# A two-layer graph kernel: final stores in source order, one weight requested by SyncE, and two weights' digit copies stored by SyncE

## The chip, the cores and the metric

The kernel runs on one core of one Trainium2 chip. That core has TensorE (PE) for matmuls, VectorE (DVE) and ScalarE (ACT) for elementwise work, GpSimd (POOL), and SyncE (SP), which in this kernel only asks for transfers. DMAs are asked for by SP, by POOL and, a few times, by ACT. The metric is the device time of one execution in microseconds (us). The kernel before was timed three times: 2391.77, 2391.25 and 2391.67 us, median 2391.67 us.

## The reference

The input x has 64 samples of 256 rows and 512 features, and all samples share one 256 x 256 adjacency matrix of zeros and ones. Layer 0 is masked attention with 8 heads, layer 1 is a product with the adjacency and then with a weight. Each ends in a residual sum and a layer norm:

```python
q, k, v = x @ Wq + bq, x @ Wk + bk, x @ Wv + bv          # 8 heads of 64
scores = q @ k.T / sqrt(64) + (1 - adj) * -1e9
x = layernorm(x + softmax(scores) @ v @ Wo + bo)
x = layernorm(x + (adj @ x) @ weight + bias)
```

## The kernel before, in words

**Tiling.** The samples are worked on in pairs, 32 pairs in all (`NP`); a pair `p` is 512 rows. Every fp32 matrix product with a weight is computed as three products of shortened operands, called digits: `high`, `low` and `diff`. A weight's digits are made once: ACT makes `high` (`split_high`, L118), DVE makes `low` and `diff` (`split_rest`, L123 and L124), and ACT scales `low` at the end (`split_scale`, L127). They are made in a ring of six SBUF tiles called `wr`, of 1 MB each, three for one weight at a time, so two weights can be there at once. From there `keep` (L129) stores each digit tile to a DRAM scratch buffer, and for all later pairs `load_w` (L105) loads them back into the ring, stage after stage. The names of the stages are `qk0`, `qk1`, `v`, `o` and `l`; `o` is the weight Wo (argument `wo`) and `l` is layer 1's weight (argument `w1`).

**Order of the work.** The issue order of PE, DVE, ACT and POOL is the order of the source: they are named in `tc.manual_schedule` (L764). Inside it `start()` handles pair 0, `first(w)` and `second(w)` are the two halves of the loop over pairs, where work on pair `w`, on pair `w - 1` and preparations for pair `w + 1` are mixed, and `ending()` handles the last pair with what remains of the one before. SP is not named there. The planner decides on its order, with its own estimates of when things are ready.

**What SP asks for.** Rows of x for the next pair come in blocks through `load_x` (L75), four DMAs of 64 KB for one block, each made of runs of 128 bytes; DVE transposes each block (`x_t`, L274). The blocks 0 and 1 of pair 1 go to tiles named `x`, the blocks 2 and 3 to tiles named `o`. The residual rows come through `load_r` (L83, 1 MB). The raw weight of layer 1 comes through `load_l` (L214). Finished rows go out at L547 and, for the last pair, at L545.

**What POOL asks for.** All loads and stores of weight digits, four DMAs of 256 KB for the raw Wo (`load_o`, L208, called at L705 in the middle of `start()`), and DMAs that add a bias to the residual rows on the way (L495, in the first and the last pairs). POOL also computes the power of minus one half in the layer norms (L523 and L595).

**Where the moved transfers are used.** Raw Wo is read first by PE at L241 (`bv_wo`, a product of the v bias with Wo), then by ACT at L118 when the digits of `o` are made in `first(1)`. The ring tiles that hold the digits of `o` are written again in `second(1)`, when the digits of `l` are made (L118 under `second(1)`); that can happen only when the stores of the `o` digits have landed. Likewise, the tiles of `l` are loaded again with `qk1` of pair 2 once the stores of `l` have landed.

**The last pair.** Its four row blocks of layer 1 are normalized by `normed` (L530): block 0 and block 2 by ACT, block 1 by DVE, and block 3 half by ACT and half by DVE. Blocks 0 to 2 and the right half of block 3 are stored by SP, the left half of block 3 by ACT. The planner has SP ask for them in the order block 1, block 0, right half of block 3, block 2. After that, all engines read a small count from memory (L782) and branch on it; the branch skips a general fallback version of the kernel. A barrier of all engines (L956) ends the program.

Of the kernel before, what the change touches and what calls it, by code (L numbers as in the profile page):

```python
# [8 lines left out]
F32 = mybir.dt.float32  # L9
# [6 lines left out]
P = 128  # L16
# [19 lines left out]
def fast(tc, x, adj, wq, bq, wk, bk, wv, bv, wo, bo, w1, b1, out):  # L36
# [6 lines left out]
    nc = tc.nc  # L43
    B, N, D = x.shape
    HD = D // H
    DC = D // P
    NC = N // P
    NP = B // 2
    HF = D // 2
# [12 lines left out]
    two = pool("two", 2)  # L62
# [8 lines left out]
    RAW, SCRATCH, W, UNCUT, BEGUN = {}, {}, {}, {}, {}  # L71
# [3 lines left out]
    def load_x(p, i):  # L75

        if p < NP:

            t = XC[p, i] = two.tile([P, D], F32, name="o" if p == 1 and i > 1 else "x")
            for q in range(4):  # L80
                nc.sync.dma_start(t[q * 32:(q + 1) * 32].rearrange("i (m j) -> i m j", j=32), xb[p, i, q])

    def load_r(p):  # L83
        if p < NP:
            t = two.tile([P, 2, NC, D], F32, name="r")
            nc.sync.dma_start(t, xr[p])
            R[p] = [t[:, b] for b in range(2)]
# [41 lines left out]
    def keep(name, i, part):  # L129

        SCRATCH[name, i] = scratch.tile([P, 2, 2, D], F32, name=f"{name}{i}")
        nc.gpsimd.dma_start(SCRATCH[name, i], part.bitcast(F32))

    def in_ring(f, name, p, k):

# [58 lines left out]
    for k in range(DC):  # L194
        RAW["v", k] = four.tile([P, D], F32, name="high")
        nc.sync.dma_start(RAW["v", k], wv[k * P:(k + 1) * P])
    for i in range(4):
        load_x(1, i)
    bo_s, b1_s = on_all(bo, "bo"), on_all(b1, "b1")

    def small_ones():
# [2 lines left out]
        nc.gpsimd.memset(first_of_32, 0.0)  # L204
        for d in range(DC):
            nc.gpsimd.memset(first_of_32[d * 32:d * 32 + 1], 1.0)

    def load_o(k):  # L208
        if k % 2 == 0:
            RAW["o"] = two.tile([P, 2, D], F32, name="hl")  # L210
        RAW["o", k] = RAW["o"][:, k % 2]
        nc.gpsimd.dma_start(RAW["o", k], wo[k // 2 * HF:(k // 2 + 1) * HF].rearrange("(h a i) e -> a h i e", h=4, a=2)[k % 2])

    def load_l():  # L214
        t = two.tile([P, DC, D], F32, name="r")
# [226 lines left out]
    def scores(p, g, between=[]):  # L442
        if not 0 <= p < NP:
            return
        for b in range(2):
            for kc in range(NC):

                sc = [banks.tile([P, 2, N], F32, name="ps") for s in range(2)]
                keys = slice(b * N + kc * P, b * N + (kc + 1) * P)
                for a in range(2):  # L450
                    digits = (1, 0, 2) if (p, g) != (0, 0) else (0,)
                    for i in digits:
                        for s in range(2):
                            r = slice(s * HD, (s + 1) * HD)
                            nc.tensor.matmul(sc[s][:, a, :], K[p, g][r, a, i, keys], Q[p, g][r, a, i, b * N:(b + 1) * N],  # L455
                                             start=i == digits[0], stop=i == digits[-1])
                if (p, g) == (NP - 1, 1):

                    names = (("x", two), ("high", four), ("low", four), ("diff", four))
                    name, pool_of = names[2 * b + kc]  # L460
                    e = [pool_of.tile([P, 2, N], F32, name=name) for _ in range(2)]
                    whole = []
                else:
                    e = one.tile([P, 2, 2, N], F32, name=f"e{2 * b + kc}")
                    whole, e = [e.rearrange("p s a n -> p (s a) n")], [e[:, s] for s in range(2)]
                E[p, g, b, kc] = e, whole
                if (b, kc) == (1, 1):
                    do(*between)
                for s in range(2):
                    nc.scalar.activation(e[s], sc[s], AF.Exp, scale=(RHO if (p, g) != (0, 0) else 1.0) * qscale)  # L470
# [15 lines left out]
    def masks(p, g, b):  # L486
        return [(masked, p, g, b, 0), (masked, p, g, b, 1), *([(summed, p, g, b)] if (p, g) != (NP - 1, 1) else [])]
# [145 lines left out]
    def do(*tasks):  # L633
        for t in tasks:
            for f, *args in (t if isinstance(t, list) else [t]):
                f(*args)
# [31 lines left out]
    def second(w):  # L668
        q, n = w - 1, w + 1
        high, rest, scale = ([(f, "l", 0, k) for k in range(DC if w == 1 else 0)] for f in (ring_high, ring_rest, ring_scale))  # L670
        values(w, 0, ([(squared, q, "o", 2), (hl_low, q, 0, 0), (hl_low, q, 0, 1), *high[:1]], [(squared, q, "o", 3), *high[1:2]]))
        scores(w, 1)
        m = masks(w, 1, 0) + masks(w, 1, 1)
        if w == 1:

            m = [high[2:] + rest[:2], m[:1] + scale[:1] + rest[2:], m[1:2] + scale[1:], m[2:3], m[3:4], m[4:]]
        else:
            m = [m[:3], m[3:4], m[4:5], [], m[5:], []]
        do((inverse, q, "o", 1), (with_b1, q, 0), m[0],
           (block, "q", n, 0), (less, q, "o", 1), (normed, q, "o", 2), (normed, q, "o", 3), m[1],  # L680
           (adj_x, q, 0, 0), (hl_high, q, 1, 0), (hl_low, q, 1, 0), m[2],
           (block, "k", n, 0), (adj_x, q, 0, 1), (hl_high, q, 1, 1), (hl_low, q, 1, 1),
           (qk_high, "q", n, 0), (qk_rest, "q", n, 0), (qk_high, "k", n, 0), (qk_rest, "k", n, 0), m[3],
           (block, "q", n, 1), (adj_x, q, 1, 0), (k_low, n, 0), (qk_high, "q", n, 1), m[4],
           (block, "k", n, 1), (stage_end, n), (adj_x, q, 1, 1), (qk_high, "k", n, 1), (qk_rest, "q", n, 1),
           m[5][:1], (block, "l", q, 0), (qk_rest, "k", n, 1), (k_low, n, 1), m[5][1:], (block, "l", q, 1), (with_b1, q, 1),
           (mean, q, "l", 0), (squared, q, "l", 0), (squared, q, "l", 1), (o_high, w, 0, 0), (o_high, w, 1, 0),
           (inverse, q, "l", 0), (o_rest, w, 0, 0), (block, "l", q, 2), (less, q, "l", 0), (o_rest, w, 1, 0),
           (block, "l", q, 3), (mean, q, "l", 1), (stage_end, q))
# [6 lines left out]
    def start():  # L696
        make_identity(nc, ident)
        do(*((x_first, i) for i in range(4)), (biases,), *((x_high, 0, i) for i in range(4)), (small_ones,))
        qk1, v = (steps_of(*stage) for stage in STAGES[:2])
        high, rest, scale = ([(f, "qk0", 1, k) for k in range(DC)] for f in (ring_high, ring_rest, ring_scale))  # L700
        do((block, "q", 0, 0), (x_rest, 0, 0), (x_rest, 0, 1), qk1[0], (block, "k", 0, 0), (x_rest, 0, 2), (x_rest, 0, 3),
           qk1[1], (block, "q", 0, 1), qk1[2], v[0], (block, "k", 0, 1), v[1][:1], (x_t, 1, 0),
           (adj_t,), qk1[3])
        scores(0, 0)
        do(v[1][1:], (x_t, 1, 1), masks(0, 0, 0), (block, "q", 0, 2), v[2], *((load_o, k) for k in range(DC)), (qk_high, "q", 0, 2), (qk_rest, "q", 0, 2), v[3], (test_adj,),  # L705
           (block, "k", 0, 2), (x_high, 1, 0), (x_high, 1, 1), (qk_high, "k", 0, 2), (qk_rest, "k", 0, 2), masks(0, 0, 1),
           (block, "q", 0, 3), (k_low, 0, 2), (qk_high, "q", 0, 3), (qk_rest, "q", 0, 3), (x_rest, 1, 0), (x_t, 1, 2),
           (block, "k", 0, 3), (stage_end, 0), (qk_high, "k", 0, 3), (qk_rest, "k", 0, 3), (x_rest, 1, 1), (x_t, 1, 3), high[:2],
           (block, "v", 0, 0), (x_high, 1, 2), high[2:], (k_low, 0, 3), (block, "v", 0, 1), (x_rest, 1, 2),
           (block, "v", 0, 2), (x_high, 1, 3), (x_rest, 1, 3), (block, "v", 0, 3), (stage_end, 0), (load_r, 0), (load_l,))  # L710
        values(0, 0)
        scores(0, 1)
        do((bv_wo,), rest[:2], scale[:1], rest[2:3], scale[1:2], rest[3:], scale[2:])
        qk0 = [(f, name, 1, j) for j in range(2) for name in "qk" for f in (qk_high, qk_rest)]
        m = masks(0, 1, 0) + masks(0, 1, 1)
        do((begun, "q", 1, 0), (begun, "k", 1, 0), (block, "q", 1, 0), m[:4], qk0[:2], (block, "k", 1, 0), m[4:5], qk0[2:4], m[5:],
           (block, "q", 1, 1), (k_low, 1, 0), qk0[4:6], (o_high, 0, 0, 0), (o_high, 0, 1, 0), (o_rest, 0, 0, 0),
           (with_bv,), (block, "k", 1, 1), qk0[6:], (stage_end, 0), (k_low, 1, 1), (o_rest, 0, 1, 0))
# [42 lines left out]
           (last_variance,), (root, 1), (less, p, "l", 1, c1), (normed, p, "l", 3, D // 2))  # L761

    PE, DVE, ACT, POOL = mybir.EngineType.PE, mybir.EngineType.DVE, mybir.EngineType.Activation, mybir.EngineType.Pool
    with tc.manual_schedule(engines={PE, DVE, ACT, POOL}):  # L764
        start()
        first(1, steps_of("o", 0))
        second(1)
        load_r(1)
        for w in range(2, NP - 1):
            first(w)  # L770
            second(w)
        ending()

    good = one.tile([P, 2, N // 32], F32, name="z")
# [186 lines left out]
```

## Time and profile before

| what | value |
|---|---|
| median of three timed runs | 2391.67 us |
| the profiled execution's own time | 2391.06 us |
| its span, first to last instruction | 2389.2 us |
| PE busy | 2374.3 us (99%) |
| DVE / ACT / POOL busy | 83% / 63% / 19% of the span |
| granted TensorE clock | 0.999 |
| DMA, mean over the span | 608.70 MB, 255 GB/s |
| DMAs asked for by POOL (q0) / by SP (q1) | 57.5% / 20.4% of 16 engines' span |
| first matmul starts / last matmul ends | 3.77 us / 2379.23 us |

The profile is of one execution, so a sum made from its rows is to be set against that execution's 2391.06 us; 1.86 us of it lie outside the span. Matmuls are pipelined and their ends are modelled, so PE's busy time alone doesn't say that it never waits: gaps between the starts of matmuls, and the waits that the views list, have to be read beside it. In the views of single instructions the columns are start, duration, engine, line, operation and tiles, and, in brackets, how long the engine stood idle and who ended it.

### The profile page before, as it was taken

How to read it: one execution, taken by the hardware profiler on the slowest of the kernel's cores; microseconds unless marked ns; L12 is line 12 of the kernel's file. 1: busy time of each engine (PE TensorE's matmuls, PEld its weight loads, DVE VectorE, ACT ScalarE, POOL GpSimd, SP SyncE). 2: the span in 40 equal slices, each digit the busy share in tenths (PEclk: the TensorE clock that was granted, in tenths of full speed). 3: DMA queues.
4: the chain of work that ended last, by engine and by line, in shares of the span. 5: the costliest groups of instructions: out<-in, count | busy, mean ns of one | idle time of the engine just before them, and what ended most of it. 6: DMA issues, size and time to landing. Idle time of an engine off the chain costs nothing.

```text
span 2389.2 us, 43002 instructions
## 1 busy us (share of the span) xinstructions
PE 2374.3 (99%) x16925; PEld 1907.5 (80%) x16925; DVE 1991.0 (83%) x3311; ACT 1505.4 (63%) x2793; POOL 443.5 (19%) x755
## 2 busy tenths in 40 slices
PE   9999999999999999999999999999999999999998
PEld 6788887888878888878888788887888878888776
DVE  7988888888888888888988888888888888888867
ACT  6666666566565665666656656666566665666655
POOL 1222111111111111121111112111111111121121
PEclk9999999999999999999999999999999999999999
DMA  9897788777888777887777967788778887777782
GB/s 295 274 310 244 265 255 283 259 230 256 260 265 271 241 237 256 264 293 238 236 255 254 310 240 224 265 255 286 258 227 261 261 264 268 238 244 255 256 274 62
DMA packets 373651, 608.70 MB, mean 255 GB/s; under 512 B 272316, under 2 KB 275908, under 8 KB 313156
## 3 DMA queue, kind: packets, MB, share of 16 engines
q0 software_dynamic: 71632, 500.21, 57.5%
q1 hardware_dynamic: 301104, 105.29, 20.4%
q8 instruction: 135, 2.21, 0.4%
q14 instruction: 72, 0.59, 0.1%
q10 hardware_dynamic: 708, 0.40, 0.1%
HBM read 551.29 MB, written 49.28 MB: 251 GB/s over the span
## 4 chain that ended last, share of the span: by engine, by line
PE 96%; DVE 1%; ACT 0%; issue 0%; POOLq 0%; ACTq 0%
PE ps L339 72%; PE ps L421 9%; PE ps L455 8%; PE ps L615 5%; PE ps L411 3%; DVE e L476 0%; DVE wr L124 0%; DVE wr L123 0%; PE ps L565 0%; DVE kT L389 0%; DVE qT L387 0%; DVE qT L385 0%; ACT kT L394 0%; DVE kT L385 0%; ACT waste L517 0%
## 5 line engine op out<-in xcount | busy, mean ns | idle before, releaser
L373 ACT ACTIVATE uncut<-ps,numbers 128x512 f32<-128x512 f32 x252 | 174.0, 690 | 274.0 <-PE ps L339 218.1
L476 DVE TENSOR_TENSOR e<-e,adjT 128x1024 f32<-128x1024 f32 x252 | 299.3, 1219 | 0.2 <-ACT e L470 0.2
L339 PE MATMUL ps<-low,wr 128*128 128x512 f32 x992 | 271.6, 395 | 0.0
L339 PE MATMUL ps<-wr,sl 128*128 128x512 f32 x1008 | 270.6, 390 | 0.1
L339 PE MATMUL ps<-wr,sh 128*128 128x512 f32 x1008 | 269.8, 389 | 0.0
L339 PE MATMUL ps<-wr,sd 128*128 128x512 f32 x1008 | 269.4, 389 | 0.0
L339 PE MATMUL ps<-high,wr 128*128 128x512 f32 x992 | 266.4, 390 | 0.0
L339 PE MATMUL ps<-diff,wr 128*128 128x512 f32 x992 | 265.0, 389 | 0.0
L523 POOL TENSOR_TENSOR ln<-ln,numbers 128x2 f32<-128x2 f32 x127 | 140.4, 1105 | 667.0 <-DVE ln L522 621.3
L470 ACT ACTIVATE e<-ps 128x512 f32<-128x512 f32 x504 | 253.3, 629 | 8.6 <-PE ps L455 8.6
L517 ACT ACTIVATE waste<-r,ln 128x512 bf16<-128x512 f32 x255 | 184.0, 722 | 104.6 <-DVE ln L510 98.9
L421 PE MATMUL ps<-e,v 128*32 128x256 f32 x4032 | 229.1, 379 | 0.0
L538 ACT ACTIVATE r<-r,ln 128x512 f32<-128x512 f32 x254 | 193.7, 811 | 55.1 <-DMA x<-in_x_dram 29.9
L339 PEld LDWEIGHTS ps<-wr,sh 128*128 128x128 f32 x1008 | 189.3, 188 | 39.9
L339 PEld LDWEIGHTS ps<-wr,sd 128*128 128x128 f32 x1008 | 189.2, 188 | 39.5 <-DMA wr<-o 0.2
L339 PEld LDWEIGHTS ps<-high,wr 128*128 128x128 f32 x992 | 186.2, 188 | 41.9 <-ACT e L470 0.8
L339 PEld LDWEIGHTS ps<-diff,wr 128*128 128x128 f32 x992 | 186.2, 188 | 39.1
L339 PEld LDWEIGHTS ps<-wr,sl 128*128 128x128 f32 x1008 | 186.9, 188 | 38.2 <-issue 0.4
L455 PEld LDWEIGHTS ps<-qT,kT 64*128 64x128 f32 x3056 | 187.8, 187 | 27.1 <-PE ps L421 12.4
L385 DVE SCALAR_TENSOR_TENSOR qT<-qT,uncut 128x512 fp32r<-128x512 f32 x126 | 86.8, 689 | 146.9 <-ACT qT L378 146.8
L339 PEld LDWEIGHTS ps<-low,wr 128*128 128x128 f32 x992 | 177.7, 188 | 35.5 <-ACT wr L127 0.6
L455 PE MATMUL ps<-qT,kT 64*128 64x256 f32 x3056 | 201.6, 285 | 0.5 <-ACT kT L394 0.5
(166 smaller groups left out, 4156.1 us busy)
## 6 DMA issues: line engine op xcount, KB each, us to landing
wr<-qk POOLq DMA_DIRECT2D x183, 1024.0 KB, 7.6
wr<-v POOLq DMA_DIRECT2D x93, 1024.0 KB, 6.8
wr<-o POOLq DMA_DIRECT2D x90, 1024.0 KB, 7.8
wr<-l POOLq DMA_DIRECT2D x90, 1024.0 KB, 8.6
r<-in_x_dram SPq DMA_DIRECT2D x32, 1024.0 KB, 12.0
out_dram<-r SPq DMA_DIRECT2D x62, 512.0 KB, 2.9
x<-in_x_dram SPq DMA_DIRECT2D x488, 64.0 KB, 5.4
qk<-wr POOLq DMA_DIRECT2D x6, 1024.0 KB, 8.3
```

The lines of the kernel that those rows point to most:

```text
L339: nc.tensor.matmul(pm, *pairs[k][i], start=i == 0 and k == 0, stop=i == n - 1 and k == DC - 1)
L373: nc.scalar.activation(to, pm, AF.Identity, bias=bias[:, j:j + 1], scale=scale)
L385: nc.vector.scalar_tensor_tensor(low, high.bitcast(F32), -RHO, UNCUT.pop((name, p, j)), op0=OP.mult, op1=OP.add)
L411: nc.tensor.matmul(at[h * 32:(h + 1) * 32, b, :], ones, chunk[h], start=i == 0, stop=i == len(sm) - 1)
L421: nc.tensor.matmul(at[h * 32:(h + 1) * 32, a, :], V[p, b][:, kc, col:col + 32], E[p, g, b, kc][0][h % 2][:, h // 2, :], start=kc == 0, sto ...
L455: nc.tensor.matmul(sc[s][:, a, :], K[p, g][r, a, i, keys], Q[p, g][r, a, i, b * N:(b + 1) * N], start=i == digits[0], stop=i == digits[-1])
L470: nc.scalar.activation(e[s], sc[s], AF.Exp, scale=(RHO if (p, g) != (0, 0) else 1.0) * qscale)
L476: nc.vector.tensor_tensor(e, e, mask[:, kc:kc + 1, :].to_broadcast([P, e.shape[1], N]), op=OP.mult)
L517: nc.scalar.activation(waste, R[p][b][:, c], AF.Square, bias=t[0][:, c:c + 1], accum_out=t[1][:, c:c + 1])
L523: nc.gpsimd.tensor_tensor(t[2], t[1], power[:, cs], op=OP.pow)
L538: nc.scalar.activation(r[:, :cut], r[:, :cut], AF.Identity, scale=scale, bias=bias)
L615: nc.tensor.matmul(pm[:, j, :], t[:, i, mc, j * P:(j + 1) * P], adjT[:, mc, :], start=mc == 0 and i == 0, stop=mc == NC - 1 and i == 1)
```

## The change

It has three parts. `keep` sends the digit stores of the stages `o` and `l` (six DMAs of 1 MB, once each in the program) to SP instead of POOL. The four DMAs of raw Wo are asked for by SP, ahead of all loops, between the blocks 0 and 1 and the blocks 2 and 3 of pair 1's rows, and `load_o` goes. `ending()` stands in a schedule of its own that also names SP, so that SP's order there is the source's too; the planner keeps SP's order everywhere before.

```diff
     def keep(name, i, part):
 
         SCRATCH[name, i] = scratch.tile([P, 2, 2, D], F32, name=f"{name}{i}")
-        nc.gpsimd.dma_start(SCRATCH[name, i], part.bitcast(F32))
+        (nc.sync if name in "ol" else nc.gpsimd).dma_start(SCRATCH[name, i], part.bitcast(F32))
...
-    for i in range(4):
+    for i in range(2):
+        load_x(1, i)
+    for k in range(DC):
+        if k % 2 == 0:
+            RAW["o"] = two.tile([P, 2, D], F32, name="hl")
+        RAW["o", k] = RAW["o"][:, k % 2]
+        nc.sync.dma_start(RAW["o", k], wo[k // 2 * HF:(k // 2 + 1) * HF].rearrange("(h a i) e -> a h i e", h=4, a=2)[k % 2])
+    for i in range(2, 4):
         load_x(1, i)
...
-    def load_o(k):
-        if k % 2 == 0:
-            RAW["o"] = two.tile([P, 2, D], F32, name="hl")
-        RAW["o", k] = RAW["o"][:, k % 2]
-        nc.gpsimd.dma_start(RAW["o", k], wo[k // 2 * HF:(k // 2 + 1) * HF].rearrange("(h a i) e -> a h i e", h=4, a=2)[k % 2])
...
-        do(v[1][1:], (x_t, 1, 1), masks(0, 0, 0), (block, "q", 0, 2), v[2], *((load_o, k) for k in range(DC)), (qk_high, "q", 0, 2), (qk_rest, "q", 0, 2), v[3], (test_adj,),
+        do(v[1][1:], (x_t, 1, 1), masks(0, 0, 0), (block, "q", 0, 2), v[2], (qk_high, "q", 0, 2), (qk_rest, "q", 0, 2), v[3], (test_adj,),
...
+    SP = mybir.EngineType.SP
     with tc.manual_schedule(engines={PE, DVE, ACT, POOL}):
         start()
         first(1, steps_of("o", 0))
...
             first(w)
             second(w)
+    with tc.manual_schedule(engines={PE, DVE, ACT, POOL, SP}):
         ending()
```

In the changed build the issue order of PE and ACT is the same as before. On POOL the ten moved DMAs are gone and the rest stands in the same order. On SP the four Wo DMAs and six digit stores come in, and the last four stores are in the order block 0, block 1, block 2, right half of block 3. On DVE two neighbours change places once, where `ending()` begins: the mean of a block of layer 1 (L510) now comes after a transpose (L428) instead of before it.

## The prediction

> **What bounds the kernel now.** I read the page's header, busy shares and chain first, then the waits by engine, then PE's gaps in stretches, and last the instructions that use what the moved DMAs bring.
>
> ```profile
> span 2389.2 us, 43002 instructions
> ...
> PE 2374.3 (99%) x16925; PEld 1907.5 (80%) x16925; DVE 1991.0 (83%) x3311; ACT 1505.4 (63%) x2793; POOL 443.5 (19%) x755
> ...
> PE 96%; DVE 1%; ACT 0%; issue 0%; POOLq 0%; ACTq 0%
> ```
>
> The chain that ended last is PE's own work for 96% of the span. Matmul starts agree with that: from the first matmul at 3.77 us to the last end at 2379.23 us, PE is without one for only 1.14 us in all. So a change of DMA queues can win at most about 1.1 us inside this stretch, and something at its end (9.97 us from 2379.23 to 2389.2); it can lose whatever it delays beyond its cover. The waits of PE between 4 and 80 us name what is left there:
>
> ```profile
> PE ps L261 <- DMA low<-in_x_dram: 4.1, 2, 3.8
> PE ps L455 <- ACT kT L394: 0.5, 1, 0.5
> ```
>
> The first is the first x rows, which are asked for before anything that moves. The second ends a stretch in which DVE is busy without a pause from 54 to 74 us, working, not waiting for a transfer.
>
> The moved transfers, from the page's list of DMA issues (queue, KB each, median us to landing), with two of SP's for comparison:
>
> ```profile
> r<-in_x_dram SPq DMA_DIRECT2D x32, 1024.0 KB, 12.0
> ...
> o<-wr POOLq DMA_DIRECT2D x3, 1024.0 KB, 5.9
> l<-wr POOLq DMA_DIRECT2D x3, 1024.0 KB, 9.8
> ...
> low<-in_x_dram SPq DMA_DIRECT2D x4, 256.0 KB, 4.2
> ...
> hl<-in_L_gnn_Wo_dram POOLq DMA_DIRECT2D x4, 256.0 KB, 13.0
> ```
>
> And the instructions that first need what they touch, from the timeline: the transpose of pair 1's block 2 (block 3's is at 45.49), PE's first use of Wo, ACT's first write of an `l` digit into the ring, and DVE's sum that needs a bias added by DMA.
>
> ```profile
> 42.24 0.71 DVE L277 STREAM_TRANSPOSE xT<-o 128x512 f32<-128x512 f32 x1
> 55.71 1.06 PE L241 MATMUL ps<-hl,numbers 128*32 128x512 f32 x8
> 113.50 0.62 ACT L118 ACTIVATE wr<-r 128x512 fp32r<-128x512 f32 x1
> 147.03 0.69 DVE L360 SCALAR_TENSOR_TENSOR r<-ps,r 128x512 f32<-128x512 f32 x1
> ```
>
> No bracket stands behind any of them: none waited.
>
> **What the Trainium skill says.** DMA: Bandwidth & Descriptors, section "Issuing engines are not separate DMA queues": DMAs of SP, ACT and POOL run on the same 16 engines, and another issuer saves only the issuing time. So the moves don't add bandwidth. The trace agrees: the DMA share is about 1.0 in every 5 us from 5 to 60 us, whoever asks. Its section "Queues, rings and completion order": each DMA engine goes round robin between the queues, a packet at a time. The trace fits: 8 KB packets of POOL's queue take 310 to 390 ns, 128 B packets of SP's 14 to 20 ns, and SP's 64 KB row pieces land after 10.9 to 16.3 us where POOL's queue is full: 32 packets per engine, each waiting for a large one, is about 11 us. A queue with small packets is thus slow beside POOL's, and that is the risk in moving stores to SP.
>
> **Part 1, Wo by SP.** POOL loses four issues of 0.69 us (32.60 to 35.31), and its store of the last `v` digit, behind them, goes out at about 32.7 instead of 35.28. It landed at 49.59, and the reload of that tile after it (50.10) was followed by PE's use at 77.23: 17 us of cover, so nothing comes of it. On SP the four stand ahead of blocks 2 and 3, bo, b1 and pair 2's blocks 0 and 1. Wo itself landed by 47.05, for a use at 55.71; now asked for at about 18.8, it lands by about 32. What is late next is x: in 2 KB packets of SP's queue (90 to 116 ns) 1 MB is 512 packets, on 16 engines 2.9 to 3.7 us alone; with POOL's packets between, about 9 us. Block 2 landed at 27.27 and moves to 30 to 37, needed at 42.24; block 3 from 32.32 to 35 to 41, needed at 45.49. At least 4.5 us are left. Without that cover each us is DVE's, which has 1.2 + 0.8 us of idle time at 49 to 54, and then PE's. bo (33.13) is needed at 71.8; pair 2's blocks (49.33 and 55.08) at 75.1, and they gain from Wo's leaving POOL's queue in front of them. Sum: 0.
>
> **Part 2, six digit stores by SP.** POOL loses six issues of about 0.55 us; behind them stand reloads that wait for PE to end a stage (97.8 and 130.2), so they go no earlier. SP is idle when the stores become ready: the `o` digits at 91.4, 95.4 and 96.6 (SP's row pieces before are issued by 90.67, the next wait for DVE until 104.73), the `l` digits at 121.6, 123.9 and 126.6. Behind these last stands pair 1's residual load, issued at 122.93 before and at about 127.1 now; it is needed at 164.5, 12 us or even 20 us after issue is early. The price of an 8 KB row on SP's queue isn't in the trace. Lower bound: it is one packet as on POOL's, and the third `o` store lands by about 105. Upper bound: it is cut to 2 KB, 32 packets per engine and store, against the 24 packets per engine of the three reloads from 99.8 us on: 24 rounds of 0.42 us end at about 110, the rest takes 0.7 us, so it lands at about 111.5. ACT needs the tile at 113.50. I take 108. Sum: 0, with 2 us of cover at the worst. For `l`, the reloads of that ring part come at 146.04; the stores land by 142 even if slow. Sum: 0.
>
> **Part 3, the end.** The order of SP's last stores becomes block 0 (ready 2379.71), 1 (2378.96), 2 (2380.97), right half of 3 (2381.72).
>
> ```profile
> 2378.98 3.94 SPq L545 DMA_DIRECT2D out_dram<-r  x4
> ...
> 2381.94 0.38 ACTq L545 DMA_DIRECT2D out_dram<-r  x1
> ```
>
> In this row before, the four issues are at 2378.98, 2379.74, 2381.75 and 2382.12; block 2 is the last, lands at 2385.41, and SP is through with its semaphores at 2386.66. New: 2379.74, 2380.1, 2381.0, 2381.75, and the last is 128 KB, as the one that landed at 2383.75. ACT's half lands at 2384.31 as before. SP would be through about 0.8 to 1.1 us earlier. But the trace also has POOL's DRAIN, from 2381.61 for 6.48 us to 2388.09, and only then the barrier opens. That one covers SP's gain wholly, unless it waits for the last store, which nothing shows. Bounds 0 and -0.9; I take -0.2.
>
> The changed place on DVE is at 2287.17: the mean (0.17) now follows the transpose (0.70), so ACT's square after it goes from 2287.43 to about 2288.0, and ACT's next two evictions move by 0.6 us, the second to an end at 2290.5. PE needs its bank for the fourth pair of score products, at 2288.64 + 3 x 0.77 = 2290.95. 0.4 us of cover. Sum: 0.
>
> Total: -0.2 us on the profiled execution's 2391.06, that is 2390.9; on the median, 0.6 higher, 2391.5. About 0.2% (4.8 us) is what a measurement can tell from no change.
>
> **Rivals.**
> 1. POOL's DRAIN follows the last landing (it ends 2.68 us after it). For: nothing else explains its length; the DRAIN at the start took 0.18. Against: it starts right after POOL's own last semaphore. Then 0.5 to 0.9 us are gained: 2391.0.
> 2. A store lands late and takes the place of what it freed (slower). Place: ACT at 113.50 waits for the third `o` store; behind it stand the evictions at 114.03 and 115.73, and PE's fourth score pair at about 116.9 needs the second (ended 116.32), so it decides from a landing at about 114.0 and then costs 1 us for 1 us. Rows that land late for 42.24 have the same form, from about 44. For: 64 KB pieces on SP took up to 20 us to land at 34 to 54. Against: the DMA engines have the same bytes to move as before and were done with this group at 112.8. If they lose 1 to 3 us: 2392.5 to 2394.5; slower by 0.2% needs a landing at 119.
> 3. The bias DMA before 147.03 landed at 146.93; queued now beside SP's stores and residual load it may land 1 us later, and PE's score pairs reuse that bank at about 148.75, 1.0 us after the sum ends. So up to 0.5 us: 2391.9. That it lands earlier gives nothing.
> 4. The 0.46 us of PE at 74 us, and the rest of the 1.14, go: 2390.6. Against: DVE's work there is the same.
>
> That the change doesn't do what it says is no rival: the issue orders of the two builds differ in just these places.
>
> **How the numbers follow.** Nothing reaches the end: 0.55, own range 2391.1 to 2392.0 (the runs spread over 0.52). Rival 1: 0.18. Rival 2: 0.12, of it 0.03 beyond 4.8 us. Rival 3: 0.08. Rival 4: 0.04. That an unseen effect of the shifted queues in the regular rounds costs more than 4.8 us: 0.02, that it gains as much: 0.01. Range 2390.4 to 2393.0: it leaves out rival 2's upper half and the unseen effects. Faster by over 0.2%: 0.01; within: 0.94; slower: 0.05.
>
> **What would show it.** PE busy 2374 us with gaps of about 1.1 us; no bracket behind the four instructions quoted above; Wo landed before 35 us; the `o` stores landed before 113; SP's four last issues between 2379.7 and 2382.1 with POOL's DRAIN still near 6.5 us. A DRAIN shorter by SP's gain is rival 1. I am wrong if ACT waits at L118 near 113.5, DVE at L277 near 42, or if PE shows gaps that recur in every round.

## The result, and the profile after

The kernel after takes 2404.27 us, the median of six executions (2403.07 to 2405.51); the kernel before, executed six times beside it, takes 2391.37 us. The ratio is 1.0052 with a 95% interval of 1.0041 to 1.0063. So it is slower by 0.5%, some 12.9 us, where 2391.5 us with a range up to 2393.0 was forecast. The profiled execution after took 2405.51 us, against 2391.06 us of the one before: 14.45 us more. One execution of the kernel before among those beside the experiments took 6164.49 us and is left out of the ratios.

From the place where `load_o` stood to the schedule, line numbers after are one higher than before (L277 is now L278). The page of the kernel after, where the header, PE's share and the chain stand:

```profile
span 2403.7 us, 42997 instructions
...
PE 2379.6 (99%) x16925; PEld 1909.2 (79%) x16925; DVE 1990.5 (83%) x3311; ACT 1502.0 (62%) x2793; POOL 435.9 (18%) x745
...
PE 97%; SPq 1%; DMA 1%; ACT 0%; DVE 0%; issue 0%; POOLq 0%; ACTq 0%; DVEq 0%
```

The chain has two members that it did not show before, SP's queue and a DMA, with 1% each after rounding. One per cent of 2404 us is 24 us, so that is the place to look. The waits of the kernel after between 40 and 80 us (engine, line, what was waited for: us in total, times, longest):

```profile
ACT high L286 <- DVE xT L278: 17.0, 1, 17.0
DVE xT L278 <- DMA o<-in_x_dram: 14.6, 1, 14.6
PEld ps L422 <- ACT v L365: 11.2, 1, 11.2
PE ps L422 <- ACT v L365: 10.7, 1, 10.7
```

Each wait occurs once, and read from the second line on they are one story: rows of x come late, DVE's transpose waits for them, ACT (L286, the first digit of these rows) for the transpose, PE for what ACT does behind that. The timeline of the kernel after shows the same instructions (start, duration, engine, line, operation; idle time before it and its releaser in brackets):

```profile
51.87 0.61 PE L422 MATMUL ps<-e,v 128*32 128x256 f32 x8
...
59.74 0.71 DVE L278 STREAM_TRANSPOSE xT<-o 128x512 f32<-128x512 f32 x1 [14.62 <-DMA o<-in_x_dram]
...
60.48 0.63 ACT L286 ACTIVATE high<-xT 128x512 fp32r<-128x512 f32 x1 [16.95 <-DVE xT L278]
61.02 1.13 ACT L118 ACTIVATE wr<-r 128x512 fp32r<-128x512 f32 x2
...
62.58 1.06 ACT L365 ACTIVATE v<-ps 128x512 f32<-128x512 f32 x2
...
63.20 5.02 PE L422 MATMUL ps<-e,v 128*32 128x256 f32 x48 [10.72 <-ACT v L365]
```

The eviction of v (L365) that PE needs has nothing to do with the late rows. It only stands behind L286 in ACT's issue order. The wait of 14.62 us on DVE becomes 10.72 us on PE.

SP's queue, from its timeline (start of the first, time until the last is issued, number of DMAs), first in the kernel before and then in the kernel after:

```profile
18.78 9.34 SPq L81 DMA_DIRECT2D o<-in_x_dram  x8
```

```profile
18.95 3.15 SPq L203 DMA_DIRECT2D hl<-in_L_gnn_Wo_dram  x4
22.15 36.72 SPq L81 DMA_DIRECT2D o<-in_x_dram  x8
```

The eight pieces of blocks 2 and 3 took SP 36.72 us to ask for instead of 9.34 us. What stands ahead of them is in the trace's records of semaphore increments:

```
load on SP (kernel after)   asked for   last increment   increments
Wo, k = 0                     18.95        25.59             5
Wo, k = 1                     19.71        35.51             5
Wo, k = 2                     20.29        45.99             5
Wo, k = 3                     20.87        52.44             5
block 2 of pair 1, 4 pieces   22.15 ...    59.12            16 each
```

A load of SP's over all 16 DMA engines shows 16 increments, one as each engine's share lands. Wo's show five: one at once, and four with data. Each of them ran on four engines, and the records fit the same four each time: the loads landed one after the other, and of the first row piece's 16 increments 12 came by 34.15, the last four from 51.73 to 53.28, about when the last of Wo landed.

On POOL's queue before, the same four loads had shown 16 increments each and landed from 46.17 to 47.05 us. That doesn't mean that each had its data on 16 engines. The increments of each load come in two groups:

```
load on POOL (kernel before)   first group        second group
Wo, k = 0                      12, to 40.60       4, from 44.19
Wo, k = 1                       8, to 41.33       8, from 44.94
Wo, k = 2                       4, to 41.65      12, from 44.45
Wo, k = 3                       none             16, from 44.72
```

This fits four engines with data for each load, but another four each time: an increment would then come late on every engine that already has the data of one of these loads to move. The same steps of 12, 8 and 4 stand in experiment 1 and in both kernels of experiment 7. So on POOL the four loads together had all 16 engines, and on SP only four. That is read from the order of the increments; no run sets the choice of engines by itself.

The granted clock is part of the loss too. The kernel after by stretches (busy us of PE, PEld, DVE, ACT, POOL with instructions in brackets, then the granted clock, the DMA share and GB/s):

```profile
52.48:57.52 5.04, 0.01 (x1) 0.00 (x0) 0.00 (x0) 0.00 (x0) 0.00 (x0) 1.00 1.02 265
57.52:63.20 5.68, 0.00 (x0) 0.00 (x0) 3.40 (x6) 2.72 (x6) 0.00 (x0) 0.50 0.70 139
63.20:67.76 4.56, 4.56 (x44) 2.18 (x48) 4.42 (x8) 2.64 (x5) 0.30 (x2) 0.50 0.62 95
```

After 5.04 us without a matmul the clock falls to half, and 4.56 us of PE's work run at it. The 48 score-times-value matmuls in the timeline above took 105 ns each (5.02 us for 48). Before, they took 57 ns each (3.64 us for 64):

```profile
49.07 3.64 PE L421 MATMUL ps<-e,v 128*32 128x256 f32 x64
```

At half speed 4.56 us hold 2.28 us of work, so by calculation this costs another 2.3 us. The Trainium skill, TensorE: Matmul & The Clock Gate, "What's actually happening", says that the clock falls after an idle window and returns after a busy one, both about 3.4 us; the trace agrees in kind, with its own 5.04 and 4.56 us. The first of the two isn't fixed: in experiments 2 and 6 the clock fell 3.0 and 2.2 us after the last matmul, sooner than the page's figure.

The sum for the two profiled executions, from gaps between matmuls and the ends:

| term | us |
|---|---|
| PE without a matmul: 11.95 instead of 1.14 | +10.8 |
| PE at half clock after the gap | +2.3 |
| other PE time (busy 2379.6 instead of 2374.3, less the 2.3) | +3.0 |
| last matmul's end, 2395.37 instead of 2379.23 | +16.1 |
| from there to the span's end, 8.29 instead of 9.97 | -1.7 |
| span | +14.5 |

The 3.0 us lie at the start: the full clock came 13.14 us after the span's start, before at 7.28 us. That most of this is chance, and where the 1.7 us of the tail come from, needed the experiments.

### The profile page after: what moved, and what is told of

Same layout as the page of the kernel before. It is cut to its first block, busy times and chain, and to the rows that moved or that the text cites. A ratio compares the mean times of both kernels' runs of the same rounds, so it can differ in the third digit from the quotient of the medians.

```text
span 2403.7 us, 42997 instructions
## 1 busy us (share of the span) xinstructions
PE 2379.6 (99%) x16925; PEld 1909.2 (79%) x16925; DVE 1990.5 (83%) x3311; ACT 1502.0 (62%) x2793; POOL 435.9 (18%) x745
## 4 chain that ended last, share of the span: by engine, by line
PE 97%; SPq 1%; DMA 1%; ACT 0%; DVE 0%; issue 0%; POOLq 0%; ACTq 0%; DVEq 0%
PE ps L340 72%; PE ps L422 9%; PE ps L456 8%; PE ps L616 5%; PE ps L412 3%; SPq L81 1%; DMA o<-in_x_dram 0%; DMA vc<-in_adj_dram 0%; DMA low<-in_x_dram 0%; SPq L203 0%; PE ps L566 0%; SPq L169 0%; ACT kT L395 0%; ACT wr L118 0%; ACT waste L518 0%
## 5 line engine op out<-in xcount | busy, mean ns | idle before, releaser
L422 PEld LDWEIGHTS ps<-e,v 128*32 128x32 f32 x4032 | 131.6, 111 | 99.1 <-ACT v L365 11.2
```

What stands on the lines that cost most here:

```text
L422: nc.tensor.matmul(at[h * 32:(h + 1) * 32, a, :], V[p, b][:, kc, col:col + 32], E[p, g, b, kc][0][h % 2][:, h // 2, :], start=kc == 0, sto ...
```

## The experiments

**1. Wo back to POOL.** All of the change but its part 1:

```diff
-    for k in range(DC):
-        if k % 2 == 0:
-            RAW["o"] = two.tile([P, 2, D], F32, name="hl")
...
-        nc.sync.dma_start(RAW["o", k], wo[k // 2 * HF:(k // 2 + 1) * HF].rearrange("(h a i) e -> a h i e", h=4, a=2)[k % 2])
...
+    def load_o(k):
...
+        nc.gpsimd.dma_start(RAW["o", k], wo[k // 2 * HF:(k // 2 + 1) * HF].rearrange("(h a i) e -> a h i e", h=4, a=2)[k % 2])
```

> Undoes the move of Wo alone; the six digit stores and the ending stay as in the changed kernel. Theory A (Wo's four DMAs on four engines each, ahead of the rows, are the whole loss): the 14.6 us wait of DVE for x rows is gone, PE has no gap over 2 us, and the time is 2389.5 to 2391.5, the lower end if the 1.6 us that the tail of the changed kernel was shorter by (8.34 against 9.97 us) belongs to SP's order at the end. Theory B (the stores by SP or the ending also cost): 2393 or more. The late grant of the full clock (13.1 against 7.3 us) should be at 7 to 8 us here if Wo on SP causes it, and can lie anywhere if it is chance.

Measured: 2391.45 us, ratio to before 0.9998 (0.9989 to 1.0006). PE's waits between 4 and 80 us in this kernel:

```profile
PE ps L261 <- DMA low<-in_x_dram: 4.2, 2, 3.9
PE ps L455 <- ACT kT L394: 0.4, 1, 0.4
PE ps L339 <- DVE numbers L272: 0.2, 1, 0.2
```

The wait for v is gone, and the whole loss with it. The stores by SP and the ending cost nothing that can be measured. The clock came at 10.5 us.

**2. Wo's move alone.** The kernel before with part 1 only.

```diff
+        nc.sync.dma_start(RAW["o", k], wo[k // 2 * HF:(k // 2 + 1) * HF].rearrange("(h a i) e -> a h i e", h=4, a=2)[k % 2])
...
-        nc.gpsimd.dma_start(RAW["o", k], wo[k // 2 * HF:(k // 2 + 1) * HF].rearrange("(h a i) e -> a h i e", h=4, a=2)[k % 2])
```

> The kernel before with the move of Wo alone (four DMAs of four engines each by SP, between blocks 1 and 2 of pair 1). Theory A (it alone is the loss): DVE waits 13 to 16 us for the rows of block 2, PE has a gap of 10 to 12 us near 52, the granted clock falls to half for a part of what follows, and the time is 2402.5 to 2406. Theory B (the stores by SP or the ending bring part of the loss): 2400 or less. On the end: if the length of POOL's DRAIN goes with the DMAs that POOL has issued, each kind giving its own part (six stores 0.49 us, four Wo loads 1.22 us, from 6.48, 5.99 and 4.77 us), it is 5.26 us here; if it goes with what SP does at the end, 6.48.

Measured: 2404.3 us (2403.48 to 2404.61), ratio 1.0051 (1.0035 to 1.0066), which is the whole change's. The waits of this kernel from 40 to 80 us:

```profile
DVE xT L278 <- DMA o<-in_x_dram: 15.7, 1, 15.7
...
PE ps L422 <- ACT v L365: 11.8, 1, 11.8
```

Part 1 is enough for the loss, and experiment 1 showed that it is needed. POOL's DRAIN, its long instruction at the barrier of all engines that ends the program (L956 before), was 5.26 us, as expected; more on that below.

**3. The same bytes, calls and place in another shape.** This tells the count of engines from the megabyte. The kernel leaves out the permutation of Wo's rows, so its output isn't the reference's.

```diff
-        nc.sync.dma_start(RAW["o", k], wo[k // 2 * HF:(k // 2 + 1) * HF].rearrange("(h a i) e -> a h i e", h=4, a=2)[k % 2])
+        nc.sync.dma_start(RAW["o", k], wo[k * P:(k + 1) * P])
```

> Four loads of 256 KB by SP in the same place, but of 128 rows of Wo in order, so that the outermost dimension of both sides is 128 and not 4. It leaves out the permutation of Wo's rows, so its output is not the reference's; the work is the same. Theory A (four engines): each of the four shows 16 increments, all have landed by 35, SP takes under 2 us over each issue behind them, block 2 of pair 1 has landed by 38, DVE doesn't wait for it over 1 us, and the time is 2389.5 to 2392. Rival M (a megabyte ahead of the rows is too much, whatever its shape): the rows still land after 45 and the time is 2396 or more.

Measured: 2389.9 us (2389.08 to 2390.33), ratio 0.999 (0.9981 to 0.9999). SP's timeline in this kernel, and DVE's transpose of block 2:

```profile
18.22 3.20 SPq L203 DMA_DIRECT2D hl<-in_L_gnn_Wo_dram  x4
21.47 12.05 SPq L81 DMA_DIRECT2D o<-in_x_dram  x8
```

```profile
43.00 0.70 DVE L278 STREAM_TRANSPOSE xT<-o 128x512 f32<-128x512 f32 x1
```

SP asks for the four loads in the same 3.2 us. But each has 16 increments, the last lands at 29.19, and the rows behind them are through SP in 12.05 us instead of 36.72. Block 2 has landed by 33.87 and block 3 by 44.13; neither transpose waits. What differs is the outermost dimension of the access pattern, and with it the order of Wo's rows, which experiment 4 keeps; it is worth the whole loss. One expectation was off: three of SP's eight issues of these rows took 2.0 to 3.2 us, not under 2.

**4. The right rows over 16 engines, as sixteen loads.**

```diff
-        nc.sync.dma_start(RAW["o", k], wo[k // 2 * HF:(k // 2 + 1) * HF].rearrange("(h a i) e -> a h i e", h=4, a=2)[k % 2])
+        o_rows = wo[k // 2 * HF:(k // 2 + 1) * HF].rearrange("(h a i) e -> a h i e", h=4, a=2)[k % 2]
+        for h in range(4):
+            nc.sync.dma_start(RAW["o", k][h * 32:(h + 1) * 32], o_rows[h])
```

> The permuted Wo by SP in the same place, but as sixteen DMAs of 32 rows (64 KB) each in place of four of 128, so that each goes over 16 engines. Theory A (four engines): the sixteen issues take SP 0.5 to 0.8 us each, some 10 us in all against 2.5, the rows of blocks 2 and 3 are asked for from about 27 and have landed by 35 and 40, needed at 42.24 and 45.49; time 2389.5 to 2392.5. Rival M (a megabyte ahead of the rows, or the time of SP over the issues): DVE waits over 3 us at the transpose of block 2 and the time is 2394 or more.

Measured: 2390.79 us (2389.68 to 2393.66), ratio 0.9996 (0.9987 to 1.0004). The two transposes of blocks 2 and 3 in this kernel (line numbers two higher than in the kernel after):

```profile
42.65 0.71 DVE L280 STREAM_TRANSPOSE xT<-o 128x512 f32<-128x512 f32 x1 [0.22 <-issue]
...
50.00 0.71 DVE L280 STREAM_TRANSPOSE xT<-o 128x512 f32<-128x512 f32 x1 [4.01 <-DMA o<-in_x_dram]
```

The time fits theory A, the rows' times don't. SP needs 12.81 us for the sixteen issues and asks for block 2 only at 32.69; it lands at 42.11, just in time, and block 3 at 49.81. PE is without a matmul for 2.61 us instead of 1.1, in pieces of at most 0.8 us. So a megabyte ahead of the rows does use up the cover, through SP's issuing time, but it is worth some 1.5 us of PE's time and not 13.

**5. The four-engine loads behind the rows.** The same four DMAs, after all four blocks of pair 1:

```diff
-    for i in range(2):
+    for i in range(4):
         load_x(1, i)
...
-    for i in range(2, 4):
-        load_x(1, i)
     bo_s, b1_s = on_all(bo, "bo"), on_all(b1, "b1")
```

> The same four Wo loads by SP, of four engines each, put behind all four row blocks of pair 1 and ahead of the two biases. Theory A (what hurts is that the rows stand behind them): the rows land by 33 as before, DVE doesn't wait for them; Wo's four land about 10 us apart, the last at 55 to 66, so that what waits now, if anything, is what reads Wo (PE near 55.7 or ACT's digits of it), by up to 10 us; time between 2390 and 2400, below the changed kernel's 2404 by at least 4. Rival (the loss comes from the traffic of Wo's four-engine loads beside the other loads and stores, not from the place): DVE still waits 8 us or more for rows and the time is 2400 or more.

Measured: 2397.18 us, ratio 1.0023 (1.0015 to 1.003). PE's timeline in this kernel:

```profile
56.25 1.05 PE L240 MATMUL ps<-hl,numbers 128*32 128x512 f32 x4
59.19 1.04 PE L240 MATMUL ps<-hl,numbers 128*32 128x512 f32 x2 [1.89 <-DMA hl<-in_L_gnn_Wo_dram]
63.05 1.88 PE L240 MATMUL ps<-hl,numbers 128*32 128x512 f32 x2 [2.81 <-DMA hl<-in_L_gnn_Wo_dram]
```

The rows are on time (35.39), and the wait sits where the slow loads are read: their data land at 38.25, 49.32, 59.15 and 63.00. Here too the clock fell to half, for 3.41 us. The loads are slow in both places. Between the blocks they made the rows behind them late as well, which cost more.

**6. Two engines.** Eight loads of 64 rows, so that the outermost dimension of the source is 2:

```diff
-        nc.sync.dma_start(RAW["o", k], wo[k // 2 * HF:(k // 2 + 1) * HF].rearrange("(h a i) e -> a h i e", h=4, a=2)[k % 2])
+        o_rows = wo[k // 2 * HF:(k // 2 + 1) * HF].rearrange("(h a i) e -> a h i e", h=4, a=2)[k % 2]
+        for h in range(0, 4, 2):
+            nc.sync.dma_start(RAW["o", k][h * 32:(h + 2) * 32], o_rows[h:h + 2])
```

> The changed kernel with Wo in the same place, but as eight loads of 64 rows in place of four of 128, so that the outermost dimension of the source is 2 and not 4. Theory A (the count of engines is the outermost dimension): each of the eight shows 3 increments, 1 and 2; the same bytes for each engine of a load, twice as many loads, so Wo's landing takes twice the 33.5 us that it took from the first issue to the last landing (18.95 to 52.44), the last near 86; the rows' wait grows by about 33 us, PE's gap from 10.7 to about 44 us, and the time is 2430 to 2445. Rival (the loss is the megabyte in SP's queue, or SP's time over the issues, not the count of engines): as the changed kernel, 2402 to 2410.

Measured: 2414.51 us (two executions), ratio 1.0097 (1.0077 to 1.0117). The waits from 40 to 80 us:

```profile
DVE xT L280 <- DMA o<-in_x_dram: 24.4, 1, 24.4
...
PE ps L424 <- ACT v L367: 21.6, 1, 21.6
```

Three increments each, as expected, and PE's gap doubled from 10.72 to 21.56 us. So for SP's loads of Wo the count of engines follows the outermost dimension of the source: two with 2, four with 4, 16 with 32 and with 128. But 44 us of gap and 2430 us had been expected. The size of my scaling was wrong: from the first issue to the last landing it took 45.5 us (21.29 to 66.80), and not twice 33.5. The intervals between landings show why:

```
load (two engines)   1      2      3      4      5      6      7      8
landed             29.71  36.07  45.34  52.12  58.78  61.43  64.08  66.80
after the one ahead        6.36   9.27   6.78   6.66   2.65   2.65   2.72
```

POOL's last transfer of this stretch landed at 57.46. Up to there 64 KB per engine took 6.4 to 9.3 us, after it 2.7. The packet records give both numbers: a packet of SP's loads is one row of 2048 B and takes 84 ns, a packet of POOL's loads and stores is 8192 B and takes 309 ns (medians). 32 packets of SP's alone are 32 x 84 ns = 2.7 us. With one of POOL's after each of them they would be 32 x (84 + 309) ns = 12.6 us. In the kernel after they took 9.9 and 10.5 us for the second and third load, which fits POOL's packets standing between most of them. So the slow landing has two parts that multiply: four engines for all of Wo instead of 16, and on each of the four 6.4 to 10.5 us beside POOL's larger packets for what takes 2.7 us alone.

**7. The ending alone, and the stores alone.** The kernel before, with one part of the change each:

```diff
+    with tc.manual_schedule(engines={PE, DVE, ACT, POOL, SP}):
         ending()
```

> The kernel before with the ending's order on SP alone. Theory D (POOL's DRAIN goes with the DMAs that POOL has issued): the DRAIN is 6.48 us as before, it still ends last, and the time is within 0.5 us of before. Rival E (the DRAIN waits for the last stores to land, so SP's earlier stores shorten it): the DRAIN is under 6.1 us and the time 0.4 to 1.0 us lower.

```diff
-        nc.gpsimd.dma_start(SCRATCH[name, i], part.bitcast(F32))
+        (nc.sync if name in "ol" else nc.gpsimd).dma_start(SCRATCH[name, i], part.bitcast(F32))
```

> The kernel before with the six stores of the digits of Wo and W1 on SP alone. Theory D: POOL's DRAIN is 5.99 us, 0.49 less than before, and the time lower by that, 0.3 to 0.6 us; no wait of over 0.5 us at ACT's first low part of Wo near 113 nor at DVE near 147. Rival E: the DRAIN stays at 6.48 us and the time is that of before. Rival S (a store by SP lands too late for the ring): PE has a gap of over 1 us between 113 and 150 and the time is 2392.5 or more.

Measured: 2392.05 us for the ending, ratio 1.0000 (0.9992 to 1.0008); 2391.61 us for the stores, ratio 0.9998 (0.9989 to 1.0006). Neither is told from before. The traces say more. The DRAIN was 6.479 us with the ending alone, as before, and 5.989 us with the stores alone. Theory D's lengths hold, E's don't. With the stores alone nothing between 110 and 150 us waited for a DMA. The `o` stores landed 3.8 to 7.1 us after their issue, the third at 104.68.

The ending alone also answers for the late clock: its build does nothing else than before for the first 2200 us, and its full clock came at 12.91 us, its last matmul ended 2.5 us later than before, PE's busy time was 2376.7 instead of 2374.3 us. Over all twelve kernels here the clock came at 7.3 to 13.1 us with no relation to the edit. So of the 3.0 us above some 2.5 are chance of that execution. Without them the two profiled executions differ by 12.0 us, against 12.9 us between the medians. Executions of before, too, spread from 2390.78 to 2394.19 us beside these experiments.

**8. What POOL's DRAIN goes with.** The kernel before with Wo by POOL as sixteen loads of 32 rows:

```diff
-        nc.gpsimd.dma_start(RAW["o", k], wo[k // 2 * HF:(k // 2 + 1) * HF].rearrange("(h a i) e -> a h i e", h=4, a=2)[k % 2])
+        o_rows = wo[k // 2 * HF:(k // 2 + 1) * HF].rearrange("(h a i) e -> a h i e", h=4, a=2)[k % 2]
+        for h in range(4):
+            nc.gpsimd.dma_start(RAW["o", k][h * 32:(h + 1) * 32], o_rows[h])
```

> The kernel before with Wo by POOL as sixteen DMAs of 32 rows in place of four of 128; nothing else. For what POOL's DRAIN goes with: if each Wo load counts alike (1.22 us for four, 0.305 each), twelve more make it 6.48 + 3.66 = 10.1 us and the time about 3.7 us longer, 2395; if it goes with packets (1.22 us for 1088), 1280 in their place make it 6.7 us and the time 2391 to 2392.5; other lengths would mean neither. POOL's twelve more issues take some 8 us at 34 to 46, ahead of its store of v's last part.

Measured: 2390.87 us (2390.36 to 2392.51), ratio 0.9997 (0.9988 to 1.0006); DRAIN 5.744 us, shorter than before. Neither expectation holds. The second was worked out from a wrong count: POOL's queue moved 71056 packets here against 71632 before, 576 fewer and not 192 more. All lengths, from the trace's records:

```
kernel                          POOL's DRAIN   POOL's packets   last matmul to end of span
before                             6.479           71632            9.97
ending alone                       6.479           71632            9.94
stores by SP alone                 5.989           70768            9.17
all but Wo's move                  5.989           70768            9.17
Wo by POOL in sixteen loads        5.744           71056            9.22
Wo's move alone                    5.259           70544            8.55
after; experiments 3, 4, 5, 6, 9   4.769           69680            7.93 to 8.37
```

The length goes with what POOL has asked for in the whole program. It doesn't follow the last store's landing: that was 3.5 to 4.0 us after the DRAIN's start in all of them. It isn't proportional to packets (5.744 us with more of them than 5.989) nor to the number of DMAs. The lengths lie about 0.245 us or twice that apart. What the DRAIN counts stays open. At 5.259 us and less it no longer sets the end alone: in the kernel after, POOL's DRAIN ends at 2402.48 and SP reaches the barrier at 2402.84, in experiment 9 at 2386.86 and 2386.76.

**9. A version without the loss.** All three parts, with Wo as sixteen loads of 32 rows, behind all of pair 1's rows:

```diff
-    for i in range(2):
+    for i in range(4):
         load_x(1, i)
     for k in range(DC):
...
-        nc.sync.dma_start(RAW["o", k], wo[k // 2 * HF:(k // 2 + 1) * HF].rearrange("(h a i) e -> a h i e", h=4, a=2)[k % 2])
-    for i in range(2, 4):
-        load_x(1, i)
+        o_rows = wo[k // 2 * HF:(k // 2 + 1) * HF].rearrange("(h a i) e -> a h i e", h=4, a=2)[k % 2]
+        for h in range(4):
+            nc.sync.dma_start(RAW["o", k][h * 32:(h + 1) * 32], o_rows[h])
     bo_s, b1_s = on_all(bo, "bo"), on_all(b1, "b1")
```

> All parts of the change, but Wo by SP as sixteen DMAs of 32 rows, behind all the rows of pair 1. Theory A: the rows land as before (by 33), Wo lands by 48 and is needed near 55, so PE has no gap over 1 us; the DRAIN is 4.77 us and the tail from the last matmul's end 8.0 to 8.5 us against 9.97; the time is 1.3 to 1.9 us below before, 2389.5 to 2390.3. Rival (SP's sixteen issues delay what it asks for behind them, the rows of the next blocks or the residual rows): a wait of over 1 us for x rows or r after 60 and the time not below before.

Measured: 2389.89 us (2389.21 to 2391.61), ratio 0.9991 (0.9983 to 1.0). SP's timeline, and PE's waits between 4 and 80 us:

```profile
18.84 9.55 SPq L81 DMA_DIRECT2D o<-in_x_dram  x8
28.43 12.48 SPq L205 DMA_DIRECT2D hl<-in_L_gnn_Wo_dram  x16
```

```profile
PE ps L262 <- DMA low<-in_x_dram: 4.1, 2, 3.8
PE ps L456 <- ACT kT L395: 0.5, 1, 0.5
PE ps L340 <- ACT e L266: 0.2, 1, 0.2
```

The rows land by 32.16, Wo by 46.01, PE is without a matmul for 1.09 us as before, and the tail is 7.93 us. Twelve of its thirteen executions lie below the lowest of before that was run beside them (2390.96). The medians differ by about 2 us, 0.09%, which is the size of the tail's 2.0 us; the interval just reaches 1, so the gain itself isn't certain.

## Why the prediction was wrong, by its own steps

**Part 1 failed, at one assumption:** "in 2 KB packets of SP's queue (90 to 116 ns) 1 MB is 512 packets, on 16 engines 2.9 to 3.7 us alone; with POOL's packets between, about 9 us". The packets had the assumed size (2048 B) and took 84 ns. The "about 9 us" was low but near for 16 engines: in experiment 3 the megabyte took 11.0 us from the first issue (18.22) to the last landing (29.19), and the prediction's own "about 11 us" for 32 packets that each wait for a large one would have said the same. "On 16 engines" was wrong. Wo's access pattern has the four groups of heads (`h=4`) outermost on the source side, and SP's DMAs spread over no more engines than that; on them the megabyte took 33.5 us. From there all followed: Wo landed at 52.44 instead of "by about 32", block 2 by 59.12 instead of "30 to 37". So "At least 4.5 us are left" became a wait of 14.6 us, and the term with "Sum: 0" measured +10.8 us of gap and +2.3 us of half clock.

The Trainium skill states the rule: DMA: Bandwidth & Descriptors, "Why a DMA increments its semaphore by 16 and not by 1". The count of engines comes from the slowest dimension that isn't 1 of both sides: it is the largest number up to 16 that divides both. For SP's and ACT's DMAs only the engines used post an increment each, and the rest of the 16 is added at once. For POOL's DMAs all 16 post, whatever the shape. The runs agree: five increments with 4, three with 2, 16 with 128 and with 32. Even the trace of the kernel before had it: ACT's loads of bias rows with 4 partitions show five increments, those with 2 rows three, while the same Wo on POOL's queue shows 16, and only their two groups tell that each load had its data on four. The prediction cited two other sections of that page and not this one.

**Even with 16 engines the cover was thinner than said.** Block 3 was forecast for 35 to 41; it landed at 44.13 with four loads (experiment 3) and at 49.81 with sixteen (experiment 4), where it cost some 1.5 us of PE's time.

**Part 2 was right.** With the stores alone the third `o` store landed at 104.68, a little ahead of the lower bound of about 105 and of the 108 that were taken, and the last `l` store at 133.03, forecast "by 142". Nobody waited.

**Part 3 was wrong in its reason and nearly right in its sum** (-0.2 us forecast; with the ending alone the tail is 9.94 us instead of 9.97). "SP would be through about 0.8 to 1.1 us earlier" didn't happen: with the ending alone SP is at the barrier 7.85 us after the last matmul, before 7.43. The last store is asked for 0.4 us earlier, 2.5 us after the last matmul instead of 2.9, but lands hardly earlier, 6.1 us after it instead of 6.2: it takes 3.6 us from issue to landing, where the one taken as its model (issued at 2381.75, landed at 2383.75) took 2.0. That the four are asked for closer together may be the reason; it isn't shown. POOL's DRAIN covers SP, as said; its length of "near 6.5" was taken as fixed and isn't. It fell by 1.7 us because ten DMAs left POOL, which the prediction had costed at nothing.

**Rival 1** (the DRAIN follows the last landing) falls: with landings 3.7 and 3.8 us after its start the DRAIN is 4.769 us in experiment 4 and 6.479 us before. **Rival 2** named the mechanism in half a sentence: "Rows that land late for 42.24 have the same form, from about 44". They did, at 59.12. It was priced at 1 to 3 us and 0.12, because the estimate of landing behind it was part 1's. Its "1 us for 1 us" is too dear for the wait alone: 14.62 us on DVE left 10.72 us on PE. But the half clock, which no case had, added 2.3. **Rivals 3 and 4** left no trace: with the stores alone nothing waits for a DMA near 147, and PE's 0.4 to 0.5 us for kT remain in experiments 1 and 9.

**The signs named beforehand** point to the place: no bracket behind DVE's L277 near 42 and Wo landed before 35 were both on the list, and neither came true.

**Left open:** what POOL's DRAIN counts, and what makes POOL's and SP's loads take different engines.

## What to carry to other kernels

Before a DMA moves from POOL to SP or ACT, look at the outermost dimension of both of its access patterns: it limits the DMA engines that work on it, and the number of increments on POOL's queue doesn't tell. Here four such DMAs in a row shared all 16 engines when POOL asked for them, and the same four engines when SP did. What such a slow DMA costs is decided by what stands behind it in its queue and on each engine that waits in order: ahead of two blocks of rows it cost some 12.9 us here, behind them some 5.4 us. Where the outermost dimension can't be changed, as with rows that go to SBUF in groups, several smaller DMAs that each spread over all engines can be faster than one large one; here sixteen in the place of four took 2390.79 us against 2404.27 us.

## What the runs showed of the hardware that was not expected

- SP can itself be held for long at one issue while transfers ahead of it haven't landed. Behind the four-engine loads four single issues of 64 KB pieces took it 5.2 to 10.2 us. It isn't peculiar to them: with Wo on POOL one issue took 8.48 us, at 40.71 in experiment 1.
- A gap on PE costs more than its length: after 2.2 to 5.0 us without a matmul (experiments 2 and 6, and the kernel after) the clock went to half, and it came back 4.6 to 4.8 us after the first matmul, which by calculation cost some 2.3 us each time. In experiment 5 two gaps of 1.89 and 2.81 us with 1.04 us of matmuls between them were enough.
- POOL's DRAIN at the end is 4.769 to 6.479 us long by what POOL asked for over the whole program. At 5.744 us and more it set the end of the span; below that SP came to the barrier within 0.5 us of it, before or after.
- The first grant of the full clock varied from 7.3 to 13.1 us after the span's start from one execution to the next, worth some 2.5 us between the kernel before and the ending alone (7.28 and 12.91 us).
